# Output stores moved from SyncE's queue to ScalarE's, in a mixture-of-experts kernel: a study of one change

## The chip, the cores and the metric

The kernel runs on one core of one Trainium2 chip. The metric is the device time of one execution in microseconds (us), as the median of several runs. Before the change it is 1002.4 us (three runs, 1000.78 to 1002.62 us).

The core has a matrix engine (TensorE, PE in the profile, with PEld for its weight loads), a vector engine (VectorE, DVE), an engine for activation functions (ScalarE, ACT), a general engine (GpSimd, POOL) and SyncE (SP), which here only issues transfers. Each engine works through its own stream of instructions in order and waits for the others by semaphores. Transfers between DRAM and the on-chip memory are issued from the queues of SP, ACT and POOL and run on 16 DMA engines.

## What is computed

The reference is a recurrent block followed by a mixture-of-experts block, both with a residual sum and layer normalisation, on 2 x 1024 tokens of 512 numbers, all in float32:

```python
def block1(x, w_hg, w_out):              # on layernorm(x)
    hidden, gate = split(x @ w_hg)
    # h_t = sigmoid(-gate) * h_(t-1) + sigmoid(gate) * g(hidden), kept in logs
    return exp(log_h) @ w_out

def block2(x, gate_kernel, w0, w1, wo):  # on layernorm(x); 8 experts, top 2
    weights, indices = top_k(x @ gate_kernel, 2)
    combine = one_hot(indices) weighted by softmax(weights)
    inter = silu(x @ w0[e]) * (x @ w1[e])       # 512 -> 1024, for each expert e
    return sum_e combine[e] * (inter @ wo[e])   # 1024 -> 512

x = x + layernorm(block1(layernorm(x)))
x = x + layernorm(block2(layernorm(x)))
```

## The kernel before the change

**The order of the work.** The program records every operation of every engine with what it reads and writes (`Program.add`, by way of a `Recorder`, so most operations have line 303). Then `schedule` sorts them: TensorE keeps its recorded order, and for every other engine a list scheduler with estimated durations picks whatever can start first. Operations marked `urgent` (the silus and the products behind them) go ahead of others that could start at the same time; `follows` keeps an operation back until others have been put in the order, without a wait on the chip; `after` and the recorded reads and writes become semaphore waits. The order is fixed when the program is built.

**Tokens and items.** The first block takes the tokens in four pieces of 512. For the second block the kernel routes each token to two experts, and GpSimd scatters its row to the experts' regions in a DRAM scratch `xs`. The 4096 rows are cut into 17 items of one expert and at most 512 rows each. Item 0 (512 columns) begins before the routing of the last tokens is known. Items 1 to 14 are the regular ones (`NR` = 14), with a width in steps of 8 that is known only at run time: TensorE's code for an item is a switch with one arm for each width, and TensorE branches into the arm through a register. Items 15 and 16 (`last`) are at most 256 wide. In the profiled execution item 7 is 136 columns wide and item 14 is 128; the other regular ones have 216 to 288.

**One item** (`run`, line 1022) has eight steps m. In each, TensorE makes two groups of four matmuls for w0 and w1 (`mm`, line 1034, on `xTi` and the weights `w`), into two pairs of banks that alternate; ScalarE takes the silu of the first (`si<-bank`), VectorE multiplies it with the second (`inter<-si,bank`); from the fifth step on TensorE also multiplies the product of four steps before with wo, into four other banks. At the end VectorE transposes these four banks into `yo`, in four parts. In the next to last step (`announce`) TensorE is given a hint on the arm of the item that follows.

**Transfers of an item.** At the first matmul of item j, `refill` (line 985) records: the weights of item j+1 (six loads of 1 MB each on SP's queue), the store of the results of item j-1 (`store`, line 969: four parts of 256 KB from `yo` to a DRAM scratch `ys`), and the rows of item j+3 (`fetch_tokens`, line 918: four loads of 256 KB, `zi<-xs_scratch`, from `xs` on SP's queue); at item 1 both items 3 and 4. Through `follows` the stores come behind the weights and the rows behind the stores. All stores of items 0 to 13 are on SP's queue; those of items 14 to 16 have two parts on SP's and two on ACT's. The rows of item 1 and item 2 are asked for during item 0 (lines 1180 and 1181).

`turn_in` (line 993) is VectorE's transpose of an item's rows from `zi` to `xTi` (`xTi<-zi`). It is recorded one item ahead: before `run` of item j the one of item j+1. There are two buffers each of `zi`, `xTi`, `yo` and of the weights.

**The end.** GpSimd gathers each token's two rows from `ys` (`gather`, line 1077); they are weighted, added, normalised and added to x (`finish`, `finish_rest`, line 1112), tile by tile of 128 tokens. The last two tiles of tokens (t >= 0 in `finish_rest`) also need the store of item 16 (`finish_late`), so they are what ends the program. Their reciprocal root comes from `mean_and_rstd`: VectorE's statistics, then a power on GpSimd.

Of the kernel before, what the change touches and what calls it, by code (L numbers as in the profile page):

```python
# [9 lines left out]
AF = mybir.ActivationFunctionType  # L10
ALU = mybir.AluOpType
# [308 lines left out]
def mingru_then_moe(nc, x, w_hg, w_out, w_gate, w0, w1, wo, out):  # L320
# [51 lines left out]
    NR = (2 * T - LEAST_A - LEAST_Z + E * (W - 1)) // W  # L372
# [4 lines left out]
    NQ = 4  # L377
    A = W // 32

    g = Program(nc)  # L380
# [19 lines left out]
    x_sb = [keep(f"x{i}", [P, D]) for i in range(TT)]  # L400
# [49 lines left out]
    for i in range(2):  # L450
        b = base + i * 48 * K
# [9 lines left out]
    v = base + 96 * K  # L461
# [31 lines left out]
    def dma(eng, dst, src, lane, nbytes, reads=None, writes=None, batch=None, after=(), follows=(), load=None):  # L493

        made = [f if callable(f) else (lambda f=f: f) for f in (dst, src)]
        return g.add(
            eng,
            lambda e: e.dma_start(made[0](), made[1]()),
            [src] if reads is None else reads,
            [dst] if writes is None else writes,  # L500
            {"POOL": 1000}.get(eng, 60),
            lane=lane,
            batch=batch,
            load=load or nbytes / 320,
            after=after,
            follows=follows,
        )
# [77 lines left out]
    def fill_gap(gaps):  # L585

        for f, *args in gaps.pop(0) if gaps else ():
            f(*args)
# [319 lines left out]
    items = [first, *regular, *last]  # L908
# [9 lines left out]
    def fetch_tokens(it, behind=(), follows=()):  # L918

        j = it.no  # L920
        at_row = register(it, "SP", ET.SP, "row", cells(it, 1), E * REG - W)
        z = z_item[j % 2]
        blocks = range(NB - 1 if it is first else NB)
        return [
            dma(
                "SP", z[ts(b, 32)],
                lambda b=b: xs[bass.ds(it.values["row"], W), ts(b, P)].rearrange("(a i) f -> i a f", i=32),
                f"z{j % 2}", W * P * 4,
                reads=[("xs", "nought", e) for e in range(E)]
                + [("xs", c, n * NT + t) for c in range(2) for n in blocks for t in range(NT)],  # L930
                batch=f"z{j}", after=[at_row, *behind], follows=follows,
            )
            for b in range(NQ)
        ]

    def fetch_weights(it, behind=(), between=lambda: ()):

        j = it.no
        gate = [register(it, "SP", ET.SP, "expert", cells(it, 0), E - 1), *behind]
        a, b, c = weights[it.weights]  # L940

        def up_half(half, follows=()):
            return [
                dma(
                    "SP", t[:, half],
                    lambda src=src: src[bass.ds(it.values["expert"], 1), :, ts(half, M // 2)].rearrange(
                        "o (p k) m -> p (o k) m", k=KD
                    ),
                    f"{name}{j % 2}{half}", D * M * 2, reads=[], after=gate, follows=follows,
                )  # L950
                for name, t, src in (("a", a, w0), ("b", b, w1))
            ]

        up_half(0)
        follows = between()
        loads = up_half(1, follows)
        for half in range(2):
            loads.append(
                dma(
                    "SP", c[:, ts(half, KM // 2), :],  # L960
                    lambda half=half: wo[bass.ds(it.values["expert"], 1), ts(half, M // 2), :].rearrange(
                        "o (k p) d -> p (o k) d", p=P
                    ),
                    f"c{j % 2}{half}", D * M * 2, reads=[], after=gate, follows=follows,
                )
            )
        return loads

    def store(it, behind=(), follows=()):

        yo, most = yo_item[it.no % 2], it.sizes[-1]
        return [
            dma(
                "ACT" if it.no >= NR and b % 2 else "SP",
                ys[it.slot * W + W - most : (it.slot + 1) * W, ts(b, P)].rearrange("(a i) f -> i a f", i=32),
                yo[ts(b, 32), A - most // 32 :].rearrange("p a c j -> p a (c j)"),
                f"yo{it.no % 2}_{b}", most * P * 4, writes=[("ys", it.slot, b)], after=behind,
                follows=() if it.no >= NR and b % 2 else follows,
            )
            for b in range(NQ)  # L980
        ]

    begun = {}

    def refill(it, op):

        j, begun[it.no] = it.no, [op]
        follows = fetch_weights(items[j + 1], [op]) if items[j + 1 : j + 2] and items[j + 1] is not last[1] else ()
        follows = store(items[j - 1], [op], follows)
        for later in items[j + 2 if j == 1 else j + 3 : j + 4]:  # L990
            fetch_tokens(later, [op], [o for o in follows if o.eng == "SP"])

    def turn_in(it, part=0, parts=1, follows=()):
        some = ts(part, A // parts)
        dst, z = xT_item[it.no % 2][:, :, some, :], z_item[it.no % 2][:, some, :]
        src = z.rearrange("p a (j k) -> p k a j", k=KD)
        g.add("DVE", lambda e: e.transpose(dst, src), [z], [dst], 3900 // parts, follows=follows)  # L997
# [24 lines left out]
    def run(it, gaps=()):  # L1022

        j = it.no
        a, b, c = weights[it.weights]
        g.item = it
        most = it.sizes[-1]
        xt = xT_item[j % 2].rearrange("p k a i -> p k (a i)")
        down = [po[0], po[1], tp[0], tp[1]]

        def mm(dst, w, rhs, first, last):
            return g.add(
                "PE",
                lambda e, n: e.matmul(dst[:, W - n : W], w, rhs[:, W - n : W], start=first, stop=last),  # L1034
                [w, rhs] if first else [w, rhs, dst], [dst], 290 if most < W else 862, columns=1,
            )

        def down_part(m, q):
            mm(down[q], c[:, m, ts(q, P)], inter[m], m == 0, m == KM - 1)

        LAG = 4
        gaps = list(gaps)
        for m in range(KM):
            p0, p1 = turn("g0", pa), turn("g1", pb)
            for dst, w in ((p0, a), (p1, b)):
                for k in range(KD):
                    o = mm(dst, w[:, m // (KM // 2), k, ts(m % (KM // 2), P)], xt[:, k, :], k == 0, k == KD - 1)
                    if j and m == k == 0 and dst is p0:
                        refill(it, o)
                fill_gap(gaps)  # L1050
            si = turn("si", si_item)
            g.ACT.activation(si, p0, AF.Silu, urgent=True)
            g.DVE.tensor_mul(inter[m], si, p1, urgent=True)
            if m >= LAG:
                for q in range(NQ):
                    down_part(m - LAG, q)
            if m == KM - 2 and it is not last[1]:
                if it is first:
                    branch(regular)
                    branch(last)  # L1060
                announce(items[j + 1])
        yo = yo_item[j % 2]

        for pair in ((0, 1), (2, 3)):
            for q in pair:
                for m in range(KM - LAG, KM - 1):
                    down_part(m, q)
            for q in pair:
                down_part(KM - 1, q)
                g.DVE.transpose(  # L1070
                    yo[:, A - most // 32 :, q, :], down[q][:, W - most :].rearrange("p (a i) -> p a i", i=32),
                    urgent=True,
                )
        g.item = None
# [37 lines left out]
    def finish_rest(i, y0, y1):  # L1112
        t = i - (TT - NT // 2)
        mean, rstd = mean_and_rstd(y0)
        g.DVE.tensor_scalar(y0, y0, mean, rstd, ALU.subtract, ALU.mult)
        g.DVE.tensor_add(
            y1.rearrange("p (c b j) -> p b c j", c=NQ, b=NQ), y0.rearrange("p (b c j) -> p b c j", c=NQ, b=NQ),
            x_sb[i].rearrange("p (c b j) -> p b c j", c=NQ, b=NQ),
        )
        dma("ACT" if t == 1 else "SP", of[ts(i, P), :], y1, f"out{i % NG}", P * D * 4, writes=[("out", i)])  # L1120


# [55 lines left out]
        ),  # L1178
    )
    fetch_weights(items[1], between=lambda: fetch_tokens(items[1]))  # L1180
    fetch_tokens(items[2])
    turn_in(items[1])
    for c in range(2):
        places(c)
    drain(list(scattered.values()))
    for it in items[1:]:
        if it is not last[1]:
            turn_in(items[it.no + 1])
        run(it)
    store(last[1])  # L1190
    gathers, late, drained = [], [], []
    for i in range(TT):
        finish(i)
# [47 lines left out]
```

## Time and profile before

| | us |
|---|---|
| median of three runs | 1002.4 |
| the profiled execution | 999.59 |
| its span, first to last instruction | 997.9 |
| first matmul | 10.2 |
| items 0 to 16 on TensorE | 283.06 to 975.25 |
| first instruction of VectorE on the last gathered rows | 987.73 |
| mean granted TensorE clock | 0.987 of full |

TensorE works nearly without a break from 10 us to the last item; from 917 us on GpSimd's gathers run beside the last two items. The groups of the page that the change touches (line, engine, operation, tiles, shapes and count; busy us and mean ns of one; idle time of the engine before them and what ended it):

```profile
L303 DVE TENSOR_TENSOR inter<-si,bank 128x512 f32<-128x512 f32 x136 | 93.4, 687 | 367.8 <-PE bank L1034 364.4
L303 ACT ACTIVATE si<-bank 128x512 f32<-128x512 f32 x136 | 81.1, 596 | 549.4 <-PE bank L1034 533.6
L997 DVE STREAM_TRANSPOSE xTi<-zi 128x2048 f32<-128x2048 f32 (+1 forms) x18 | 66.1, 3671 | 12.1 <-DMA zi<-xs_scratch 12.1
```

Both ScalarE and VectorE sit idle most of the time until TensorE's banks are ready. The transfers (KB of each, median us from issue to landing):

```profile
w<-in_L_ffn_w_kernel_dram SPq DMA_DIRECT2D x64, 1024.0 KB, 8.4
wo<-in_L_ffn_wo_kernel_dram SPq DMA_DIRECT2D x32, 1024.0 KB, 13.9
zi<-xs_scratch SPq DMA_DIRECT2D x68, 256.0 KB, 5.5
ys_scratch<-yo SPq DMA_DIRECT2D x58, 256.0 KB, 10.1
```

### The profile page before, as it was taken

The page shows a single profiled execution, that of the slowest core. Times are in us where ns is not written, and L with a number is a line of the kernel's source. Part 1 is how long each engine was busy: PE and PEld are TensorE (multiplying, and loading weights), DVE is VectorE, ACT ScalarE, POOL GpSimd, SP SyncE. Part 2 cuts the span into 40 slices and gives each one's busy share as a digit, 9 for nine tenths or more (in the row PEclk, how much of TensorE's full clock was granted, in tenths as well). Part 3 has the DMA queues.
Part 4 walks back from the last instruction along what each step waited for, and adds up shares of the span by engine and source line. Part 5 has one row for each costly group of instructions (what it writes and reads, how often), then busy time and mean ns, then how long its engine had stood idle before and what let it go on. Part 6 is the DMA issues. An engine that isn't in the chain of part 4 may idle for free.

```text
span 997.9 us, 11029 instructions
## 1 busy us (share of the span) xinstructions
PE 957.3 (96%) x4134; PEld 721.4 (72%) x4134; DVE 442.8 (44%) x948; ACT 155.0 (16%) x269; POOL 111.1 (11%) x146
## 2 busy tenths in 40 slices
PE   6999999999999999999999999899999999998990
PEld 4444454555445448888899999787799988898990
DVE  6643737564555952323314314322224323144875
ACT  2322020212112001011011011111011110111230
POOL 3200104014213000000000000000000000001671
PEclk9999999999999999999999999999999999999996
DMA  9920002002911489667395595946385793856673
GB/s 301 393 85 1 0 1 85 0 1 105 293 67 75 124 225 338 169 213 258 86 334 188 153 335 206 336 139 248 91 293 168 218 320 84 274 183 193 186 239 112
DMA packets 143372, 177.55 MB, mean 178 GB/s; under 512 B 6192, under 2 KB 79920, under 8 KB 143280
## 3 DMA queue, kind: packets, MB, share of 16 engines
q1 hardware_dynamic: 134368, 156.53, 48.8%
q0 software_dynamic: 5280, 17.31, 5.3%
q10 hardware_dynamic: 3632, 2.36, 0.9%
q8 instruction: 73, 1.20, 0.5%
q14 instruction: 19, 0.16, 0.1%
HBM read 136.33 MB, written 39.85 MB: 177 GB/s over the span
## 4 chain that ended last, share of the span: by engine, by line
PE 93%; DVE 2%; DMA 2%; issue 1%; POOL 1%; ACT 0%; SPq 0%; POOLq 0%
PE bank L1034 65%; PE bank L303 28%; DMA got<-ys_scratch,where_i 1%; DVE got L303 1%; DVE little L303 1%; POOL little L303 1%; DMA ys_scratch<-yo 0%; DMA x<-in_L_attn_x_dram 0%; DMA got<-ys_scratch,table_e 0%; POOL got L1081 0%; DVE inter L303 0%; DVE yo L303 0%; DVE xn_in L303 0%; ACT got L303 0%; ACT xT L303 0%
## 5 line engine op out<-in xcount | busy, mean ns | idle before, releaser
L1034 PE MATMUL bank<-xTi,w 128*128 128x256 f32 (+11 forms) x2176 | 463.8, 371 | 8.4 <-issue 8.3
L1034 PEld LDWEIGHTS bank<-xTi,w 128*128 128x128 f32 x2176 | 386.6, 191 | 71.6 <-issue 37.6
L303 DVE TENSOR_TENSOR inter<-si,bank 128x512 f32<-128x512 f32 x136 | 93.4, 687 | 367.8 <-PE bank L1034 364.4
L1034 PE MATMUL bank<-inter,wo 128*128 128x256 f32 (+11 forms) x1088 | 234.8, 369 | 1.1 <-DVE inter L303 1.1
L1034 PEld LDWEIGHTS bank<-inter,wo 128*128 128x128 f32 x1088 | 192.9, 190 | 32.9 <-issue 14.6
L303 PE MATMUL bank<-xT,whg 128*128 128x512 f32 (+1 forms) x400 | 171.3, 579 | 0.2 <-ACT xT L303 0.2
L303 ACT ACTIVATE si<-bank 128x512 f32<-128x512 f32 x136 | 81.1, 596 | 549.4 <-PE bank L1034 533.6
L303 PEld LDWEIGHTS bank<-xT,whg 128*128 128x128 f32 x400 | 74.1, 191 | 77.4 <-issue 75.6
L1081 POOL DMA_INDIRECT got<-ys_scratch,where_i x28 | 29.2, 1043 | 603.8 <-DMA ys_scratch<-yo 592.9
L303 PE MATMUL bank<-wout,h 128*128 128x512 f32 x192 | 84.2, 595 | 0.0
L997 DVE STREAM_TRANSPOSE xTi<-zi 128x2048 f32<-128x2048 f32 (+1 forms) x18 | 66.1, 3671 | 12.1 <-DMA zi<-xs_scratch 12.1
L303 PEld LDWEIGHTS bank<-wout,h 128*128 128x128 f32 x192 | 35.9, 190 | 43.2 <-issue 41.1
L303 POOL TENSOR_TENSOR little<-little,few 128x1 f32<-128x1 f32 x64 | 38.9, 613 | 220.2 <-DVE little L303 216.0
L303 DVE STREAM_TRANSPOSE yo<-bank 128x512 f32<-128x512 f32 (+1 forms) x68 | 46.2, 679 | 26.7 <-PE bank L1034 23.1
L303 DVE SCALAR_TENSOR_TENSOR s<-bank,s 128x512 f32<-128x512 f32 x24 | 16.6, 691 | 78.5 <-ACT s L303 78.4
L704 POOL DMA_INDIRECT xs_scratch<-y,row_i x32 | 33.5, 1047 | 47.5 <-DVE little L303 33.7
L303 ACT ACTIVATE z<-bank 128x512 f32<-128x512 f32 x24 | 14.3, 597 | 109.5 <-PE bank L303 109.5
L303 DVE BATCH_NORM_STATS2 little<-x 128x6 f32<-128x512 f32 x32 | 21.7, 682 | 7.8 <-DMA x<-in_L_attn_x_dram 7.3
L303 ACT ACTIVATE s<-bank 128x512 f32<-128x512 f32 x24 | 14.3, 597 | 57.0 <-PE bank L303 57.0
L303 PEld LDWEIGHTS bank<-wg,yT 128*128 128x128 f32 x128 | 16.4, 192 | 5.3 <-issue 5.3
L303 PEld LDWEIGHTS bank<-ident,xn_in 128*128 128x128 f32 x64 | 8.7, 155 | 15.2 <-DVE xn_in L303 8.8
L303 PE MATMUL bank<-ident,xn_in 128*128 128x128 f32 x64 | 11.1, 303 | 8.0 <-DVE little L303 7.8
(127 smaller groups left out, 330.2 us busy)
## 6 DMA issues: line engine op xcount, KB each, us to landing
w<-in_L_ffn_w_kernel_dram SPq DMA_DIRECT2D x64, 1024.0 KB, 8.4
wo<-in_L_ffn_wo_kernel_dram SPq DMA_DIRECT2D x32, 1024.0 KB, 13.9
zi<-xs_scratch SPq DMA_DIRECT2D x68, 256.0 KB, 5.5
ys_scratch<-yo SPq DMA_DIRECT2D x58, 256.0 KB, 10.1
xs_scratch<-nought SPq DMA_DIRECT2D x8, 1024.0 KB, 12.6
out_dram<-got SPq DMA_DIRECT2D x15, 256.0 KB, 3.7
x<-in_L_attn_x_dram SPq DMA_DIRECT2D x14, 256.0 KB, 7.9
whg<-in_L_attn_w_hg_dram SPq DMA_DIRECT2D x10, 256.0 KB, 6.4
```

The lines of the kernel that those rows point to most:

```text
L303: return program.add(eng, lambda e: getattr(e, name)(*args, **kw), ins, [out], ns, urgent=urgent)
L704: lambda e, c=c, i=i: e.indirect_dma_start(xs, bass.IndirectOffsetOnAxis(ap=row_i[:, c, i : i + 1], axis=0), y_of[i], None),
L997: g.add("DVE", lambda e: e.transpose(dst, src), [z], [dst], 3900 // parts, follows=follows)
L1034: lambda e, n: e.matmul(dst[:, W - n : W], w, rhs[:, W - n : W], start=first, stop=last),
L1081: lambda e: e.indirect_dma_start(dst, None, source, bass.IndirectOffsetOnAxis(ap=rows, axis=0)),
```

## The change

It has three parts.

1. `store` takes the engines as an argument. For items 0 to 13 it is no longer called in `refill` but in `run` of the item behind, in the fifth step, with ACT alone: part b is kept in the order behind the silu of step b+1 (`silus[m - NQ + 1 :]`), so the four parts stand behind silus 1 to 4 of the item. Items 14 to 16 store through SP and ACT as before. In `refill` the rows then follow the weights directly.
2. The rows of item 2 are no longer asked for during item 0. `refill` of item 1 asks for items 2 and 3, and just behind it the turn of item 2 and the loads of item 4's rows are recorded.
3. For the last two tiles `finish_rest` takes the mean off first (it doesn't need the power), with the reordering of columns in that instruction, and then multiplies by the reciprocal root and adds x in one instruction. Before, one instruction took off the mean and multiplied, and a second added x and reordered.

```diff
-    def store(it, behind=(), follows=()):
+    def store(it, engines, behind=(), follows=None):
 
         yo, most = yo_item[it.no % 2], it.sizes[-1]
-        return [
+        for b in range(NQ):
             dma(
-                "ACT" if it.no >= NR and b % 2 else "SP",
+                engines[b % len(engines)],
...
-                follows=() if it.no >= NR and b % 2 else follows,
-            )
-            for b in range(NQ)
-        ]
+                follows=follows[b] if follows else (),
+            )
...
         j, begun[it.no] = it.no, [op]
-        follows = fetch_weights(items[j + 1], [op]) if items[j + 1 : j + 2] and items[j + 1] is not last[1] else ()
-        follows = store(items[j - 1], [op], follows)
-        for later in items[j + 2 if j == 1 else j + 3 : j + 4]:
-            fetch_tokens(later, [op], [o for o in follows if o.eng == "SP"])
+        loads = fetch_weights(items[j + 1], [op]) if it not in last else ()
+        if it in last:
+            store(items[j - 1], ("SP", "ACT"), [op])
+        for later in items[2:4] if j == 1 else items[j + 3 : j + 4]:
+            fetch_tokens(later, [op], loads)
...
         LAG = 4
-        gaps = list(gaps)
+        gaps, silus = list(gaps), []
...
                     if j and m == k == 0 and dst is p0:
                         refill(it, o)
+                        if j == 1:
+                            turn_in(items[2])
+                            fetch_tokens(items[4], [o])
                 fill_gap(gaps)
             si = turn("si", si_item)
-            g.ACT.activation(si, p0, AF.Silu, urgent=True)
+            o = g.ACT.activation(si, p0, AF.Silu, urgent=True)
+            silus.append([o])
+            if j and it not in last and m == NQ:
+                store(items[j - 1], ("ACT",), begun[j], silus[m - NQ + 1 :])
...
         mean, rstd = mean_and_rstd(y0)
-        g.DVE.tensor_scalar(y0, y0, mean, rstd, ALU.subtract, ALU.mult)
-        g.DVE.tensor_add(
-            y1.rearrange("p (c b j) -> p b c j", c=NQ, b=NQ), y0.rearrange("p (b c j) -> p b c j", c=NQ, b=NQ),
-            x_sb[i].rearrange("p (c b j) -> p b c j", c=NQ, b=NQ),
+        y0_v, x_v, y1_v = (
+            v.rearrange(how, c=NQ, b=NQ)
+            for v, how in (
+                (y0, "p (b c j) -> p b c j"), (x_sb[i], "p (c b j) -> p b c j"), (y1, "p (c b j) -> p b c j"),
+            )
         )
+        if t >= 0:
+            g.DVE.tensor_scalar(y1_v, y0_v, mean, None, ALU.subtract)
+            g.DVE.scalar_tensor_tensor(y1, y1, rstd, x_sb[i], ALU.mult, ALU.add)
+        else:
+            g.DVE.tensor_scalar(y0, y0, mean, rstd, ALU.subtract, ALU.mult)
+            g.DVE.tensor_add(y1_v, y0_v, x_v)
...
     fetch_weights(items[1], between=lambda: fetch_tokens(items[1]))
-    fetch_tokens(items[2])
     turn_in(items[1])
...
         if it is not last[1]:
-            turn_in(items[it.no + 1])
+            if it.no > 1:
+                turn_in(items[it.no + 1])
         run(it)
-    store(last[1])
+    store(last[1], ("SP", "ACT"))
```

## The prediction, made before the changed kernel was built or run

> **What bounds the kernel now.** I read the busy shares and the chain that ended last, then who made TensorE wait, then TensorE's timeline, and last the windows of the stretches where it stood still. The busy shares, and the chain by engine:
>
> ```profile
> PE 957.3 (96%) x4134; PEld 721.4 (72%) x4134; DVE 442.8 (44%) x948; ACT 155.0 (16%) x269; POOL 111.1 (11%) x146
> ...
> PE 93%; DVE 2%; DMA 2%; issue 1%; POOL 1%; ACT 0%; SPq 0%; POOLq 0%
> ```
>
> TensorE is the bound from 14.8 us to 943.7 us. What holds TensorE itself (us in total, times, longest):
>
> ```profile
> PE bank L1034 <- issue: 8.3, 5, 3.4
> PE bank L303 <- DVE little L303: 7.8, 2, 7.7
> PE bank L1034 <- DVE inter L303: 1.1, 1, 1.1
> ```
>
> No row names the store or the tokens' loads, and the silus do not appear. The only idle time inside the items is 8.3 us put down to "issue". The timeline of TensorE has four of those five places:
>
> ```profile
> 607.77 9.52 PE L1034 MATMUL bank<-xTi,w 128*128 128x136 f32 x80 [0.58 <-issue]
> ...
> 632.98 20.81 PE L1034 MATMUL bank<-xTi,w 128*128 128x280 f32 x80 [2.71 <-issue]
> ...
> 909.10 14.94 PE L1034 MATMUL bank<-xTi,w 128*128 128x192 f32 x80 [3.41 <-issue]
> ...
> 943.67 12.73 PE L1034 MATMUL bank<-xTi,w 128*128 128x184 f32 x80 [1.43 <-issue]
> ```
>
> Each is the first matmul of an item. The two long ones follow the two narrowest regular items: item 7, 136 columns, 607.77 to 630.27, and item 14, 128 columns, 884.09 to 905.69. The trace's records of TensorE's sequencer show why. At each item's end it takes a branch into the next item's code, and 12 of the 16 branches (those after items 1 to 6 and 8 to 13) take 2.63 to 3.21 us, mean 2.8. At 256 columns the branch starts 3.2 us before the last matmul ends (410.24 against 413.47), so it is hidden. After items 7 and 14 it starts only 1.42 and 1.39 us before (628.85 and 904.30) and also takes longer, 3.97 and 4.64 us. 3.97 + 0.16 of start - 1.42 = 2.71: the whole gap. The code comes in DMA packets of 16 KB on q8. In those 12 items the last packet before the branch's own starts 5.6 to 12.5 us ahead of the branch; in the two narrow items it starts at 628.56 and 904.91, beside the branch, and the target's own packet follows only 1.81 and 1.50 us later. The branch ends some 2.5 us after that.
>
> The windows around these places (columns: PE, PEld, DVE, ACT, POOL busy, granted clock, DMA share, GB/s):
>
> ```profile
> 623.00:628.00 5.00, 5.00 (x45) 5.00 (x44) 2.91 (x3) 0.60 (x1) 0.00 (x0) 1.00 1.06 375
> 628.00:633.00 5.00, 2.29 (x21) 2.10 (x19) 4.68 (x5) 0.00 (x0) 0.00 (x0) 1.00 0.94 264
> 633.00:638.00 5.00, 5.00 (x14) 3.77 (x15) 0.29 (x1) 0.60 (x1) 0.00 (x0) 0.66 0.98 264
> ...
> 900.00:905.00 5.00, 5.00 (x47) 5.00 (x47) 3.67 (x2) 0.60 (x1) 0.00 (x0) 1.00 1.09 367
> 905.00:910.00 5.00, 1.59 (x12) 1.42 (x11) 3.58 (x5) 0.00 (x0) 0.00 (x0) 1.00 0.24 63
> 910.00:917.00 7.00, 7.00 (x35) 7.00 (x34) 1.35 (x2) 1.19 (x2) 0.00 (x0) 0.76 0.65 150
> ```
>
> The 16 DMA engines are full up to the branch, and after each long gap the clock is halved: 0.66 over 5 us and 0.76 over 7 us are both 3.4 us at half speed, 1.7 us lost. So each long gap costs itself and 1.7 us more; after the gap of 1.43 us the clock stayed at 1.00.
>
> SP's timeline in item 7 shows the order in its queue (start, length, issues):
>
> ```profile
> 608.43 3.07 SPq L498 DMA_DIRECT2D w<-in_L_ffn_w_kernel_dram  x4
> ...
> 611.60 4.85 SPq L498 DMA_DIRECT2D wo<-in_L_ffn_wo_kernel_dram  x2
> ...
> 616.50 10.87 SPq L498 DMA_DIRECT2D ys_scratch<-yo  x4
> ...
> 627.55 4.70 SPq L498 DMA_DIRECT2D zi<-xs_scratch  x4
> ```
>
> **The change part by part.** The sum is made on the profiled execution: span 997.9 us, 999.59 us with 1.7 us around it; the median of the runs is 1002.4 us, 2.8 us above it.
>
> *Stores leave SP's queue.* 10 to 11 us of SP's time per item go (10.87 us above). No TensorE wait names SP's loads, so in the 14 items this is worth 0. It is hidden behind the items' matmuls, 21.6 to 47 us each. The tokens' loads are then issued some 10 us earlier; their turn on DVE comes one item later, so that is 0 too.
>
> *Stores enter ScalarE's queue,* four issues of 256 KB behind silus 1 to 4. Behind each stands the next silu, for that silu DVE's product, and for both the bank that TensorE fills two steps on. The trace has ScalarE issue two such stores only once:
>
> ```profile
> 909.71 2.66 ACTq L498 DMA_DIRECT2D ys_scratch<-yo  x2
> ```
>
> 0.37 us, then 2.27 us. On SP the median is 2.57 us and the longest 5.07 us. In a wide item silus are 3.46 us apart at first, so 0.60 + 2.57 fits. In item 7 they are 1.86 us apart (five steps in 9.52 us, less the tail), then 2.79. Counting from the end of the first gate group, with every later issue s: silu 2 ends at 4.32, silu 4 at 4.32 + 2s + 1.2 and must end by 12.1, silu 5 at 4.32 + 3s + 1.8 and must end by 14.9. Up to s = 2.93 nothing is late. At 5.07 silus 3 to 5 come 0.7, 2.9 and 2.9 us late, 6.4 us per narrow item, 12.8 in all. Bounds 0 and +12.8; I take 0, because SP's median lies under 2.93 and ScalarE's second issue too.
>
> *What the code packets meet.* Per DMA engine item 7 has 192 weight packets of 2 KB (84 to 88 ns each, 16.5 us), 128 store packets and 128 token packets of 512 B (27 to 28 ns, 3.5 us each). They fill the engines from 609.8 to past 632 in whatever order. Today one queue sends weights until 626.3, then stores, then tokens. With stores on ScalarE's queue from some 612 us, they mix with the weights, which then end near 626.3 + 3.5 = 629.8. The late packet at 628.56 would thus meet weights instead of stores. In item 14 the weights would end near 905.5 instead of 902.5. Price: under weights a code packet began 1.46 and 1.59 us after the hint that asks for it (622.01 to 623.47, 897.74 to 899.33); in item 11 without load 0.48 (785.20 to 785.68; in others another packet comes between), so a load of weights costs about 1 us. I take +0.9 for item 7, and +0.4 for item 14, where the drain is nearly over. Bounds: the branch at its undisturbed 2.8 us shortens the gaps by 1.2 and 1.8 to about 1.5 each, and at 1.43 the clock was not halved, so -(3.0 + 3.4) = -6.4; a second queue that doubles the excess costs +3.0. Taken: **+1.3**.
>
> Here the Trainium skill speaks against the change. "DMA: Bandwidth & Descriptors", section on queues, rings and completion order, says that an engine goes round its queue rows packet by packet; with ScalarE's row beside SP's the code's row would get every third turn instead of every second. The 0.48 against 1.5 us above is the only row here that bears on it; by the rule the excess of 1 us would double in both items, +2.0 in place of +1.3.
>
> *Third item's rows.* Four loads and DVE's turn (3.87 us) leave item 0, where DVE waited 7.22 us for them at 361.96 to 369.19; TensorE had no gap there, so the gain is 0. In item 1 the rows now follow the weights: 372.8 + 16.5 + 3.5 (stores) + 3.5 puts them near 396, and the turn must start by 413.5 - 3.9 = 409.6. Reserve 13 us; beyond it each us is paid in full. On DVE the turn may stand ahead of the four transposes of item 1 (3.1 us); their banks are filled again only some 17 us later. The fifth item's rows on SP wait for that turn, with the next weights behind them; those wait for item 2's first matmul, which needs the same turn. 0.
>
> *Last rows.* The end of DVE's timeline:
>
> ```profile
> 990.89 0.15 DVE L303 TENSOR_SCALAR little<-little 128x1 f32<-128x1 f32 x1
> 991.38 1.16 DVE L303 TENSOR_SCALAR got<-got,little,little 128x512 f32<-128x512 f32 x2 [0.34 <-POOL little L303]
> 992.46 1.29 DVE L303 TENSOR_TENSOR got<-got,x 128x512 f32<-128x512 f32 x2
> ```
>
> Two subtractions move into the 0.34 us wait for the power. Then DVE is busy from 991.04: two subtractions (1.16, or 1.29 with the reordered write), two fused multiply-adds (751 ns each in the row of that operation at 987.73, overlapping 0.1): end at 993.6 to 993.8 instead of 993.75. Bounds -0.15 and +0.1: **-0.1**.
>
> Sum: 0 + 0 + 1.3 + 0 - 0.1 = +1.2: span 999.1, and on the runs' median **1003.6 us**.
>
> **The rivals.** *ScalarE is held (slower).* For it: SP's stores took up to 5.07 us in a full queue, and the weights' packets share the engines; if packets alternate, a store needs 32 x (84 + 28) = 3.6 us. Then silus 4 and 5 of each narrow item come 0.6 and 1.4 us late, 4.0 us in all, with the sum above +5.2: 1007.6. It decides from s = 2.93 us on. Against: the lone 2.27 us. *The code is fetched later (slower).* The excess doubles, +3.0 instead of +1.3, -0.1: 1005.3; more if both queues are full at each request. For it: both long gaps lie where the engines are full. Against: the total bytes are the same. *The gaps close (faster).* If the mix lets the code through, -6.4 - 0.1: 995.9; one gap alone, 1.2 + 1.7 = 2.9, gives 999.4. For it: 512 B packets hold an engine 28 ns, weights 84, and a mix is shorter on average than weights alone when the earlier packets (623.47, 899.33) are asked for. Against: weights then last longer.
>
> Of the clock, the Trainium skill ("TensorE: Matmul & The Clock Gate", part 1, the HAM clock gate) says that it falls after an idle window of about 3.4 us that runs free. Here a gap of 2.71 us was enough. By the rule alone only the 3.41 us gap is sure to pay, and the rival would gain 1.7 us less.
>
> *The change does not do what it says:* if the hand-made order puts the stores elsewhere than behind silus, it is the first rival with another silu.
>
> **How the numbers follow.** Near no change 0.37, ScalarE held 0.22, code later 0.14, gaps close 0.27. Forecast 1003.6; its own range is 1001 to 1005. 0.2% (2.0 us) is about what a measurement of this kernel can tell from no change. Faster: 0.25 of the gaps' case and 0.02 of the forecast's; slower: 0.33 of the two slower cases and 0.04 of the forecast's; the rest, 0.36, is same. Range 997 to 1008: it leaves out the full close of both gaps and the far end of ScalarE's bounds.
>
> **What would show it.** Right: the gaps at the starts of items 8 and 15 still 2.5 to 4.5 us with a halved clock after each, TensorE whole inside items 7 and 14, ScalarE's issues under 2.9 us, DVE's last step 0.1 us nearer to the power. Wrong: idle time before matmuls inside items 7 or 14 put down to ScalarE or DVE's product, or a branch back at 2.8 us and the clock at 1.00 at 633 and 910.

## The result and the profile after

The changed kernel takes 1019.4 us (median of six runs, 1018.5 to 1020.8) where the kernel before, in six runs beside it, took 1001.8: a ratio of 1.0176, with a 95% interval of 1.0163 to 1.0189. The change costs 17.6 us. The forecast was 1003.6, and its range ended at 1008.

The profiled execution has a span of 1018.2 us against 997.9, 20.3 us more; that is above the 17.6 of the medians because the profiled execution of the kernel before, 999.59 us, lies 2.2 us under its median. On TensorE the difference falls as follows; "item" is the time from its first matmul to the first matmul of the next.

| stretch | before, us | after, us | difference |
|---|---|---|---|
| up to the first matmul of item 1 | 372.03 | 372.24 | +0.2 |
| item 1 | 41.44 | 55.17 | +13.7 |
| items 2 to 6 | | | -0.5 |
| item 7 and the gap behind it | 25.21 | 28.99 | +3.8 |
| item 8 | 47.06 | 47.38 | +0.3 |
| items 9 to 14 | | | +0.8 |
| item 15 and the gap behind it | | | +1.5 |
| item 16 and the end | | | +0.5 |

Two thirds of this difference are in item 1, in which the moved rows of item 2 are now fetched, and most of the rest is behind item 7. The 1.5 us of item 15 are not followed up; in the run last_only below, which leaves the transfers there as they were, that stretch is 0.8 us longer too. The chain by engine, from the page of the changed kernel, and what made TensorE wait (total, times, longest; line 1033 is now that of the items' matmuls):

```profile
PE 88%; DVE 4%; issue 3%; DMA 2%; SPq 2%; POOL 1%; ACT 0%; ACTq 0%; DVEq 0%; POOLq 0%
```

```profile
PE bank L1033 <- issue: 13.3, 6, 6.5
PE bank L1033 <- DVE inter L303: 12.7, 2, 11.6
PE bank L303 <- DVE little L303: 7.9, 2, 7.7
```

TensorE's share of the chain fell from 93% to 88%. The second row was 1.1 us, once; now one wait of 11.6 us stands in it, a wait for VectorE's product. The first row grew from 8.3 to 13.3 us. ScalarE's silus are not among the rows. The timeline of item 1 after the change (start, length, engine, instruction, in brackets the idle time before and what ended it):

```profile
380.83 25.33 SPq L498 DMA_DIRECT2D zi<-xs_scratch  x12
...
400.31 3.79 DVE L996 STREAM_TRANSPOSE xTi<-zi 128x2048 f32<-128x2048 f32 x1 [16.75 <-DMA zi<-xs_scratch]
...
404.02 1.24 DVE L303 TENSOR_TENSOR inter<-si,bank 128x512 f32<-128x512 f32 x2
404.71 3.78 PE L1033 MATMUL bank<-xTi,w 128*128 128x256 f32 x8 [11.59 <-DVE inter L303]
```

Read it from the bottom. TensorE stopped at 404.71 - 11.59 = 393.12, in the sixth step of the item, because the bank that it was to fill still held the second group of the fourth step, which VectorE had not multiplied. VectorE had done three products by 383.56 and then stood for 16.75 us in front of the turn of item 2, whose rows landed at 400.3. The fourth and fifth products stood behind that turn and came at 404.02. So the moved rows are not late for item 2: their turn ended at 404.1, and without the gap item 2 would have begun near 413.7. They are late for item 1, through VectorE's order. With the long gap the granted clock was also halved, for 10.24 us (398.29 to 408.53), of which 3.82 us were work: another 1.9 us.

Behind item 7 and item 14, TensorE's timeline; then SP's and ScalarE's queues in item 7:

```profile
650.21 21.13 PE L1033 MATMUL bank<-xTi,w 128*128 128x280 f32 x80 [6.49 <-issue]
...
927.42 14.89 PE L1033 MATMUL bank<-xTi,w 128*128 128x192 f32 x80 [3.68 <-issue]
```

```profile
624.87 6.34 SPq L498 DMA_DIRECT2D wo<-in_L_ffn_wo_kernel_dram  x2
629.86 0.31 ACTq L498 DMA_DIRECT2D ys_scratch<-yo  x1
631.39 10.69 SPq L498 DMA_DIRECT2D zi<-xs_scratch  x4
```

The gap behind item 7 went from 2.71 to 6.49 us, the one behind item 14 from 3.41 to 3.68. TensorE's branch into item 8 took 7.76 us (642.29 to 650.05) where it took 3.97. Its code packets on q8 started at 642.32 and 647.21, 4.9 us apart, where before they were 1.81 us apart. ScalarE issues such a store in 0.31 to 0.37 us and is not held by it: the stores are spread over the item (one of the four is shown), and TensorE is whole inside items 7 and 14. But weights of 2 KB and stores of 512 B now share the DMA engines, some 150 packets of each per us, and 98% of the weights' packets have begun by 642.7 instead of 626.7, 2.6 us later counted from the item's first matmul (which is itself 13.5 us later). The rows behind them fall at 642.8 to 650, over the branch. Counted from the item's first matmul the rows begin only 1 us earlier than before (21.5 us, against 22.6 by the count of packets); what changed is that the second code packet, which came just as the stores ended before, now comes when rows have been running for over 4 us.

The windows there (PE, PEld, DVE, ACT, POOL busy, granted clock, DMA share, GB/s):

```profile
642.00:647.00 5.00, 1.72 (x15) 1.52 (x14) 4.42 (x5) 0.00 (x0) 0.00 (x0) 1.00 1.16 228
647.00:652.00 5.00, 1.79 (x4) 1.41 (x5) 0.00 (x0) 0.00 (x0) 0.00 (x0) 0.55 0.46 74
```

In the first window the engines are full with TensorE idle from 643.7; the clock falls at 647.46, before the work comes back, and stays at half for 6.83 us, two times the 3.41 us of before. As 2.75 us of that lie in the gap, item 8 pays only 0.3 us more than it did.

The end of VectorE's timeline after the change:

```profile
1012.15 0.75 DVE L303 SCALAR_TENSOR_TENSOR got<-got,little,x 128x512 f32<-128x512 f32 x1 [0.43 <-POOL little L303]
1012.82 0.15 DVE L303 TENSOR_SCALAR little<-little 128x1 f32<-128x1 f32 x1
...
1013.04 0.72 POOL L303 TENSOR_TENSOR little<-little,few 128x1 f32<-128x1 f32 x1 [1.00 <-DVE little L303]
1013.87 0.75 DVE L303 SCALAR_TENSOR_TENSOR got<-got,little,x 128x512 f32<-128x512 f32 x1 [0.51 <-POOL little L303]
```

The small instruction at 1012.82 is what the second tile's power waits for. It stands behind the first tile's multiply-add, so the power starts at 1013.04, after POOL had been idle for a whole microsecond, and VectorE then waits 0.51 us for it. Before, the two powers ran back to back:

```profile
990.78 1.18 POOL L303 TENSOR_TENSOR little<-little,few 128x1 f32<-128x1 f32 x2 [4.13 <-DVE little L303]
```

From the first instruction on the last gathered rows to VectorE's last end it is 6.40 us (1008.22 to 1014.62) instead of 6.02 (987.73 to 993.75).

### The profile page after: what moved, and what is told of

Its sections match the earlier page's. It is cut to its first block, busy times and chain, and to the rows that moved or that the text cites. A ratio compares the mean times of both kernels' runs of the same rounds, so it can differ in the third digit from the quotient of the medians.

```text
span 1018.2 us, 11031 instructions
## 1 busy us (share of the span) xinstructions
PE 960.8 (94%) x4134; PEld 722.8 (71%) x4134; DVE 442.3 (43%) x948; ACT 155.1 (15%) x269; POOL 109.9 (11%) x146
## 4 chain that ended last, share of the span: by engine, by line
PE 88%; DVE 4%; issue 3%; DMA 2%; SPq 2%; POOL 1%; ACT 0%; ACTq 0%; DVEq 0%; POOLq 0%
PE bank L1033 62%; PE bank L303 26%; SPq L498 2%; DVE little L303 1%; DVE got L303 1%; DMA zi<-xs_scratch 1%; POOL little L303 1%; DVE inter L303 1%; DMA ys_scratch<-yo 0%; DVE xTi L996 0%; DMA x<-in_L_attn_x_dram 0%; DMA got<-ys_scratch,where_i 0%; DMA got<-ys_scratch,table_e 0%; DVE yo L303 0%; DVE xn_gru L303 0%
## 5 line engine op out<-in xcount | busy, mean ns | idle before, releaser
L1033 PE MATMUL bank<-xTi,w 128*128 128x256 f32 (+11 forms) x2176 | 466.7, 372 | 25.0 <-issue 13.3
```

## Experiments

Each ratio is to the kernel before, run in turns on the same chip, with its 95% interval; gaps and branches are read from one profiled execution of each kernel. The line of the items' matmuls is 1033, 1034 or 1035, as the edit has it.

### Which part does it: the parts taken apart

Four kernels, timed together; the kernel before took 1002.7 us beside them.

*The second part undone (rows_back).* All of the change but the rows of item 2:

```diff
-        for later in items[2:4] if j == 1 else items[j + 3 : j + 4]:
+        for later in items[j + 2 if j == 1 else j + 3 : j + 4]:
...
-                        if j == 1:
-                            turn_in(items[2])
-                            fetch_tokens(items[4], [o])
...
+    fetch_tokens(items[2])
     turn_in(items[1])
...
-            if it.no > 1:
-                turn_in(items[it.no + 1])
+            turn_in(items[it.no + 1])
```

> The changed kernel with its second part undone: item 2's rows are asked for in item 0 again and its turn stands there. Theory (VectorE's turn of item 2 was put ahead of the product of step 4 in item 1 and waits there for rows that land 28 us after the item's start): TensorE's gap of 11.59 us and the half clock behind it go, item 1 is 41.4 us instead of 55.2, the median falls by 13.7 to 1005.7 us. Rival (the wait is for a queue that is late anyway through the stores on ScalarE, and moves to another wait): less than 5 us of the 13.7 come back, over 1014 us.

1006.0 us, 1.0036 [1.0022, 1.0051]. No gap in item 1; behind item 7 it is still 6.3 us. So some 14 of the 17.6 us belong to the second part (1.0176 against 1.0036).

*The turn behind the products (turn_last).* All parts stay, and the rows of item 2 are still asked for in item 1; only the turn and the loads of item 4 stand behind the last product of item 1:

```diff
-                        if j == 1:
-                            turn_in(items[2])
-                            fetch_tokens(items[4], [o])
...
-            g.DVE.tensor_mul(inter[m], si, p1, urgent=True)
+            o = g.DVE.tensor_mul(inter[m], si, p1, urgent=True)
+            if j == 1 and m == KM - 1:
+                turn_in(items[2], follows=[o])
+                fetch_tokens(items[4], begun[1])
```

> All three parts kept, but the turn of item 2 and the loads of item 4's rows are kept in the order behind the product of step 8 of item 1. Theory (only the place of the turn in VectorE's order costs; the rows land in time): 1005.7 us as with the rows put back, no gap in item 1 and none at the start of item 2. Rival (the rows come too late for item 2 because of the load on the DMA engines in item 1): a gap of several us at the first matmul of item 2, over 1010 us.

1006.4 us, 1.0042 [1.0025, 1.0060]: as rows_back, with no gap in item 1 nor at item 2. Its longest wait of an item's matmul for a product:

```profile
PE bank L1033 <- DVE inter L303: 1.4, 1, 1.4
```

The late rows by themselves cost nothing that can be measured; the place of the turn in VectorE's order costs all of it.

*The first part alone (stores_only)*: `store` with its engines, called behind the silus, on the kernel before:

> The kernel before with the first part alone (stores of items 0 to 13 on ScalarE's queue behind silus 1 to 4). Theory (the stores take turns with the weights, so that the weights end 17 us later than before in item 7's terms at 642 instead of 626 and the rows' loads lie over the branch into item 8): the gap at the start of item 8 is about 6.5 us instead of 2.71, item 7 with it 29 us instead of 25.2, the median 1001.8 + 5.5 = 1007.3 us or somewhat less. Rival (the longer branch comes from the other parts or from the shift in time of item 7): gap 2.7, 1002 us.

1005.2 us, 1.0029 [1.0019, 1.0039]: +2.9 us, about half of the 5.5 us that were expected. The gap behind item 7 is 6.1 us in it, near the 6.5 expected. Counted from the item's first matmul the weights end 2.8 us later in it than in the kernel before, not 17.

*The third part alone (last_only)*: the two branches of `if t >= 0` in `finish_rest`, on the kernel before:

> The kernel before with the third part alone (mean taken off beside the power, one fused instruction behind it, for the last two tiles). Theory (the order made by the planner puts the first tile's subtraction ahead of the second tile's statistics and the fused instruction ahead of the second tile's power, which costs more than the 0.34 us wait that it fills): from VectorE's first instruction on the last gathered rows to its last 6.4 us instead of 6.0, the median +0.4, 1002.2 us. Rival (as predicted): 5.9 us, -0.1.

1003.3 us, 1.0008 [0.9999, 1.0018]: not told apart from no change by the time. In the trace VectorE takes 6.38 us from the first instruction on the last gathered rows, against 6.02: the third part costs 0.36 us there, where it was to save 0.1. The traces of the other kernels without it (stores_only, rows_only, clear7) have 6.03 to 6.06.

### Item 1: is it the planner's duration?

*The second part alone (rows_only)*: what rows_back undid, put into the kernel before, with the stores still on SP's queue:

> The kernel before with the second part alone: item 2's rows asked for in item 1, all stores still on SP's queue ahead of them. Theory (the turn's place in VectorE's order and the time at which its rows land decide, not the queue of the stores): the planner now puts the turn behind the product of step 4 instead of step 3, the rows land some 3 us later than in the changed kernel, and TensorE waits for the product of step 5: a gap of 5 to 12 us in item 1 with a half clock behind it, 1008 to 1016 us. Rival (only the stores beside the rows on a second queue make them late): a gap under 3 us, under 1005 us.

1012.2 us, 1.0117 [1.0096, 1.0138]. Its timeline of item 1:

```profile
402.62 3.79 DVE L998 STREAM_TRANSPOSE xTi<-zi 128x2048 f32<-128x2048 f32 x1 [14.93 <-DMA zi<-xs_scratch]
...
407.04 3.43 PE L1035 MATMUL bank<-xTi,w 128*128 128x256 f32 x8 [8.05 <-DVE inter L303]
```

The same wait without the other parts. Here the turn stands one product further back, so TensorE got one step further (398.99 instead of 393.12) and lost 8.05 us instead of 11.59, though the rows came 1.6 us later counted from the item's first matmul (29.7 against 28.1).

Why the turn stands there can be read from the order that the program itself makes. Its scheduler takes 290 ns for a matmul of the last two items, whose sizes are under 512, and 862 ns for every other, as if all 512 columns were filled. An item has 8 x 8 + 8 x 4 = 96 matmuls: 82.8 us by that estimate, 41.4 us on the chip (432 ns each). With 862 ns the scheduler has the rows of item 2 land 25.9 us after the item's first matmul and the fourth product ready only 29.1 us after it (440.8 and 444.05 against 415.0 in its own time), and puts the turn first. On the chip the rows land 28.1 us after the first matmul and the fourth product was due by 20.9.

*A nearer duration (planner).* One number of the changed kernel:

```diff
-290 if most < W else 862
+290 if most < W else 440 if j else 862
```

> The changed kernel, all three parts, with one number of the planner changed: its estimate for a matmul of a regular item is 440 ns (about what one takes at 256 columns) in place of 862 ns (512 columns); item 0 keeps 862. Theory (the planner saw item 1 as 86 us long instead of 41, so 25 us, at which it expected the rows, fell ahead of the product of step 4): the turn now stands behind the product of step 6 and no product waits long enough to hold TensorE, 1005 to 1007 us. Rival (the planner's times do not matter, the turn waits wherever it stands): a gap of several us in item 1, 1010 us or more.

1007.1 us, 1.0053 [1.0036, 1.0071]; the ratio of the changed kernel was 1.0176. The turn now stands behind the sixth product, TensorE has no gap in item 1, and the gap behind item 7 is 5.6 us. Its longest wait for a product:

```profile
PE bank L1033 <- DVE inter L303: 1.9, 1, 1.9
```

With one estimate put near the measured duration the loss of the second part is gone. This is shown, then, from both sides: the place moved by hand, and the number that chose the place.

### The gap behind item 7: the rows or the second queue

In item 7 two things changed: weights and stores alternate (theory B: a second full queue delays the code), and the rows' loads fall over the branch (theory A). Two kernels, both with the second part undone, take one of them away. In rows7_later the rows of item 10 are asked for in item 8, and both queues stay full in item 7. In stores7_later item 6's stores go in item 8, and the rows stay.

```diff
# rows7_later
-        for later in items[j + 2 if j == 1 else j + 3 : j + 4]:
+        for later in items[j + 2 if j in (1, 8) else j + 3 : j + (3 if j == 7 else 4)]:
# stores7_later
-                store(items[j - 1], ("ACT",), begun[j], silus[m - NQ + 1 :])
+                for i in (6, 7) if j == 8 else (j - 1,) if j != 7 else ():
+                    store(items[i], ("ACT",), begun[j], silus[m - NQ + 1 :])
```

> The changed kernel with the second part undone (gap at the start of item 8: 6.3 us there), and item 10's rows asked for in item 8 instead of item 7, so that item 7 has weights and stores alone. Theory A (the branch's code waits behind loads of rows, 512 B reads from DRAM): the gap falls to 2 to 3.5 us and the half clock to one window, 1000.5 to 1002.5 us. Theory B (it waits because two queues are busy in place of one, whatever they carry): the gap stays at 5 us or more, 1005 us.

> The same with the rows left in item 7 and the stores of item 6 moved behind the silus of item 8, so that in item 7 one queue alone is busy: weights until some 16.5 us after its start, then rows, which then lie over the branch. Theory A (loads of rows hold the code): the gap stays at 4 us or more, 1003 us or more. Theory B (two busy queues): it falls to 2.7 us or less, 1000 to 1002 us.

The kernel before took 1001.1 us beside these two. rows7_later: 1000.9, 0.9997 [0.9985, 1.0010]. stores7_later: 1004.5, 1.0029 [1.0017, 1.0040]. The first matmul of item 8 in the one and in the other:

```profile
633.81 20.81 PE L1033 MATMUL bank<-xTi,w 128*128 128x280 f32 x80 [3.07 <-issue]
```

```profile
635.65 21.17 PE L1033 MATMUL bank<-xTi,w 128*128 128x280 f32 x80 [5.40 <-issue]
```

With two queues and no rows the gap is 3.07 us (branch 4.33) and the whole loss of the first part is gone; with one queue and the rows over the branch (626.5 to 634) it is 5.40 (branch 6.61). In the kernel before, the rows stood behind the stores in the one queue, and the code packets met the stores. Theory A holds. For B these traces leave nothing that can be told apart: the 3.07 us lie within what the same gap takes in the kernels that store from SP's queue in item 7 (2.41 in last_only, 2.71 in the kernel before, 3.23 in rows_only). Why loads of rows hold the code back and stores do not, no run here shows.

The same can be read behind item 0, where the branch is hidden. In the eight kernels that ask for item 2's rows in item 0 and leave the hint in its place, row packets run over that branch and it takes 5.1 to 6.1 us; in the four that ask for them in item 1 (the changed kernel, turn_last, planner, rows_only) it takes 2.7 to 3.2.

*Both moved (clear7).* Both edits above, with the third part undone as well. Item 7 then issues neither stores nor rows:

> Stores of regular items on ScalarE's queue, second and third part undone; item 6's stores and item 10's rows both moved from item 7 to item 8, so that the branch behind item 7 meets DMA engines that have done the weights. Theory (the code's packets are late only through other transfers): the branch takes 2.8 us, the gap at the start of item 8 is about 1.5 us and the clock stays whole there, 2.9 us less than the kernel before: 998 to 999 us with 0.3 more at item 15. Rival (a narrow item's branch is long in itself): the gap stays at 2.7 us or more, 1001 us.

```profile
632.08 19.12 PE L1033 MATMUL bank<-xTi,w 128*128 128x280 f32 x80 [1.45 <-issue]
```

999.3 us against 1002.5, 0.9972 [0.9960, 0.9983]. The branch is back at 2.72 us, the gap at 1.45, and the clock stays whole: the 80 matmuls take 19.12 us where they took 20.81 before. The gap that the prediction's third rival wanted closed can be closed to 1.45 us, by keeping stores and rows out of the item ahead of it.

*The same for item 14 (clear7_14):* item 13's stores go in item 15, two of its four parts on each queue.

```diff
-            store(items[j - 1], ("SP", "ACT"), [op])
+            for i in (13, 14) if j == 15 else (15,):
+                store(items[i], ("SP", "ACT"), [op])
...
-                for i in (6, 7) if j == 8 else (j - 1,) if j != 7 else ():
+                for i in (6, 7) if j == 8 else (j - 1,) if j not in (7, 14) else ():
```

> The same, and item 13's stores moved from item 14 to item 15, so that the branch behind item 14 meets idle DMA engines too. Theory: the gap at the start of item 15 falls from 3.4 to about 1.5 us without a half clock, another 3.6 us less: 995 us; the gathers, which wait for twice the stores, begin some 5 us later and end ahead of item 16's store all the same. Rival (the gathers' later start reaches the end): 998 us or more.

998.9 us, 0.9962 [0.9949, 0.9976], 3.6 us of the 7 expected; the intervals of this kernel and of clear7 overlap, so the second step is not shown to gain anything. Both gaps are down to 1.73 and 1.56 us with the clock whole, but item 15 now begins with eight stores:

```profile
905.60 5.43 ACTq L498 DMA_DIRECT2D ys_scratch<-yo  x4
...
911.73 8.07 PE L1034 MATMUL bank<-xTi,w 128*128 128x192 f32 x48 [1.28 <-ACT si L303]
```

Here ScalarE is held: four issues in a row take 5.43 us, the silu behind them is late, and TensorE waits 1.28 us for it. This is the wait of the prediction's first rival. ScalarE was also held in item 8 of clear7, where two stores stand behind each silu: one such pair took 4.66 us and a silu came about 1 us late, but no TensorE wait followed. The rival that was recorded for this run, gathers that begin later and reach the end, asked for 998 us or more, and the trace bears it out in part: the first gather begins at 917.9 instead of 915.4 in clear7, the chain that ended last now runs through the gathers, and of the 2.9 us by which TensorE ends earlier than in clear7 (971.8 against 974.7) 1.8 are left at the end of the span. Both kernels beat the one before, but which items are narrow is known only at run time, so they fit these data alone.

### Asking for the code earlier

*The hint two steps earlier (hint_early)*, on the kernel before:

```diff
-if m == KM - 2 and it is not last[1]:
+if m == KM - 4 and it is not last[1]:
```

> The kernel before with TensorE's hint on the next item's code two steps earlier (fifth step instead of seventh). Theory (in the narrow items the hint's own packet comes so late that the branch's packet stands behind it): the packet starts some 3 us or more ahead of the branch, both branches fall to 2.8 us, both long gaps to 1.5 us without half clocks, 996 us. Rival (the packet waits for the block of code that is fetched in sequence, not for the hint): gaps of 2.5 us or more, 1001 to 1003 us.

1078.1 us, 1.0771 [1.0737, 1.0805]. The theory fell. What TensorE waited for in it:

```profile
PE bank L1034 <- issue: 51.1, 15, 5.8
```

The gaps of 2.2 to 5.8 us are now at 15 places: almost every item start has two branches that fetch, the first of them of 3.3 to 4.7 us where it took 0.3 to 0.5 before. Another 15.7 us are one wait in item 0, for VectorE; it is put down to the tables that the branch's register needs, which the program reads where it gives the hint. Why the code is gone again after two more steps no trace here shows.

## Why the prediction was wrong, step by step

**The third item's rows: the step that failed.** "On DVE the turn may stand ahead of the four transposes of item 1 (3.1 us); their banks are filled again only some 17 us later." It stood ahead of the last five products. The step measured the lateness of the rows against the start of item 2 ("the turn must start by 409.6", "Reserve 13 us") and not against the next thing in VectorE's order, the fourth product, which TensorE needed at 393.1. The rows came at 400.3 where 396 was worked out, so even the predicted time was past that point. What was missed is the order: the step didn't work out where the scheduler would put the turn among the products, which follows from the 862 ns that it takes for these matmuls. Price: 0 was taken; the second part measured +11.7 us alone (1.0117) and some 13 in the changed kernel (1.0176 against 1.0042). No rival named it, so the range was too short by its size.

**What the code packets meet: right place, wrong traffic, and so the wrong size.** The sum had +1.3, with +3.0 as the upper bound and rival. Measured: +2.9 us by the times [1.9 to 3.9], 4.1 us in the profile of the change (3.78 for item 7 and its gap, 0.32 for item 8). The step priced the late packet under weights and stores, and let the drain of the weights go from 626.3 to 629.8, 3.5 us later, where the trace has 2.6. It didn't follow that shift to the next in the queue: the rows, which then lie over the branch. It was the branch's second packet that came late, 4.9 us behind the first instead of 1.81, and not the first one that the step priced. The step also gave the rows the 27 to 28 ns a packet of the stores; there they took 42 to 74 ns (means of each us, 643 to 649), and rows had taken about as long in the kernel before behind item 0 (50 to 56 ns, 363 to 368). At item 14, where no rows follow (there is no item 17), the gap grew by 0.27 us in the profiles (+0.4 was taken).

The rule that was weighed there, the Trainium skill's "DMA: Bandwidth & Descriptors" (queues, rings and completion order), that queues are served in turn packet by packet, agrees with item 7 in that weights and stores went in equal numbers, 150 + 150 packets per us. The estimate by it was +2.0 in place of +1.3. But the experiments put the lengthened gap on the rows: with two full queues and no rows the gap behind item 7 is 3.07 us, within the 2.41 to 3.23 of the kernels that store from SP's queue there.

**ScalarE's issues: right.** 0 was taken; the issues behind silus 1 to 4 take 0.31 to 0.37 us and no silu of item 7 or 14 is late. The bound of 12.8 us had its price from a queue with weights ahead, which ScalarE's queue hasn't. The same for SP's freed time: worth 0.

**The last rows: wrong sign, small.** -0.1 was taken, +0.36 measured. The step counted VectorE's instructions as one run from 991.04 on, and took the order as it was. But the first tile's multiply-add, ready as soon as its power is, was put ahead of the second tile's small instructions, and so the second power came late.

**The gaps.** "still 2.5 to 4.5 us with a halved clock after each" held for item 15's start (3.68) and not for item 8's (6.49). The 1.7 us of halved clock that each long gap was given are not fixed: a gap of 3.23 us in rows_only lost none. The sign was left open, with slower at 0.37.

## What to carry to other kernels

A moved instruction is late or early against what stands behind it on its engine, not only against its own user: find the place that the scheduler gives it, from the durations that the scheduler believes, before costing it at nothing. When a transfer is made longer, follow the shift through its queue to what lands beside the next critical fetch. An instruction split to fill a wait can push another tile's way to the same unit back.

## What the runs showed of the hardware

- A branch whose code has to be fetched took 2.6 to 3.3 us with quiet DMA engines, 3.7 to 4.9 us beside stores and weights (behind items 7 and 14), and 5.1 to 7.8 us beside row loads of 512 B (behind items 0 and 7).
- The halved clock comes in pieces of 3.41 us: two of them after every gap of 5.4 to 8.05 us, three after 11.6, and no gap up to 2.12 us was followed by one. Between 2.2 and 3.2 us it goes either way: gaps of 2.24 (hint_early), 2.41 (last_only) and 2.71 us (the kernel before) lost a piece, gaps of 2.85 (hint_early) and 3.23 us (rows_only) lost none. The Trainium skill's "TensorE: Matmul & The Clock Gate" (part 1, the HAM clock gate) has a free-running idle window of about 3.4 us; the pieces agree with it, while gaps well under that were enough to lose one.
- Four stores of 256 KB issued in a row held ScalarE for 5.43 us (clear7_14), two behind one silu for up to 4.66 us (clear7); issued one by one behind silus they took 0.31 to 0.37 us each.
- The place of the hint on a branch's target matters: given two of eight steps earlier, the kernel took 7.7% longer.
